# A routed expert's first rows: one expert's input gathered by one-hot matrix products on the chip instead of through memory

## The chip, the cores and the metric

The kernel runs on one core of a Trainium2 chip. A core has five engines with an instruction queue each: TensorE (PE, matrix products into PSUM; its weight loads are listed as PEld), VectorE (DVE), ScalarE (ACT), GpSimd (POOL) and SyncE (SP, which here only starts transfers). They wait for each other through semaphores. Data lies in memory (DRAM), in SBUF (128 partitions) and in PSUM, which holds the results of products. Transfers run on 16 DMA engines; SP and POOL start them.

The metric is the time of one execution on the device in microseconds (us). Everything is computed in 32-bit floating point; TensorE runs such a product of two full operands as two passes, so the profile counts two records for each.

## The reference

The model is a block of three layers over 16 sequences of 256 tokens with 128 features, 4096 tokens in all: half of a mixture of experts, an attention block, and half of the same mixture again, each on the layer-normalised stream `x` and added to it.

```
x = x + 0.5 * moe(layernorm(x))
x = x + attention(layernorm(x))      # delta rule in chunks of 32, three long convolutions, a gate
x = x + 0.5 * moe(layernorm(x))
```

What matters here is the mixture of experts, `moe`. There are 8 experts. Every token takes the two with the largest gate probability, k = 0 and k = 1. Each expert has room for 640 tokens per k; a token's place is the number of earlier tokens that chose the same expert, and a token whose place is 640 or more is dropped.

```
onehot = (eid[:, None] == experts[None, :])
pos = cumsum(onehot, axis=0) - 1 at the token's expert;  valid = pos < capacity
disp = zeros((E, capacity, D)).at[eid, pos].add(x)
gate = silu(disp @ wi_gate);  up = disp @ wi_up;  expert_out = (gate * up) @ wo
out += weight * expert_out[eid, pos]          # where valid
```

## The kernel before

**Staging.** The 4096 tokens are four groups g of 1024, each held as 128 partitions of 8 tiles n (NG = 4, NC = 8). The first mixture is layer 1, the second is layer 2. In between stands the attention phase, in which each group goes through nine or so strands (front, systems, scan, conv, gate, routing and so on). The strands are Python generators. A planner (class Weave) merges them by estimated costs and due times into one order for every engine, which is then kept as written. The last group's gate and routing are split in two halves of four tiles.

**Routing.** `choose` normalises the rows of a group into a tile `row` (128 features, the token's number, two weights), transposes them, multiplies with the gate's weights and finds the two experts. `place` turns the choices into places: VectorE sums over tiles (L462), TensorE counts over partitions in three products into `pp` (L473 to L479), and VectorE makes the number of a slot per token and k (L482 to L500: `bb`, `pos`, `full`, `place`, `send`). A slot number is 640 e + pos. Then `dispatch` (L531) writes the rows to the memory tensor `disp` at these slots: one indirect DMA by GpSimd for each tile and k. The slots were filled with zero rows beforehand. For k = 0 the eight scatters of a group go out at once. Those of the last two groups for k = 1 (`rest`) are kept for the time of the experts.

**Experts.** `experts` runs 16 steps in layer 2, k = 0 with e = 0 to 7, then k = 1. Three steps are fetched ahead. For each step SP loads the weights `we` (L233) and the slots of the expert (`fetch`, L608) as `xd`: 128 partitions of 5 rows, where slot 5 p + j is at partition p, part j. `expert` transposes the five parts on TensorE (`ptx`, L635) and copies the result to `xdT`, 128 features by 640 slots, three parts by ACT (L638) and two by DVE (L640). Then come eight pairs of products of 320 columns, `pg` and `pu` (L648, L653), with Silu on ACT and a multiplication on DVE, and 20 products back to 128 features, `py` (L668). The results are weighted to `ye` (L679) and scattered to the tokens' rows by GpSimd (L693).

**The seam.** The first expert of layer 2 can begin when the eight scatters of the last group for k = 0 have landed and SP has fetched its slots. SP has the first three weight loads, then three fetches in its queue at that point; all these fetches wait for all scatters to the tensor. GpSimd has four memsets, the eight scatters, and then the first four of `rest`. On ACT a table load for Silu (`ready`) stands before the first expert's copies. PSUM is one pool of five general banks (tag G) and three others in the attention phase, and another pool of eight for the experts.

Of the kernel before, what the change touches and what calls it, by code (L numbers as in the profile page):

```python
# [14 lines left out]
P = 128  # L15
# [143 lines left out]
def macaron_kernel(ctx: ExitStack, tc: tile.TileContext, x_in, consts, wts, w1b, wexp, out):  # L159
# [91 lines left out]

    eps_ln = one.tile([P, 1], F32, name="eps_ln")
    nc.vector.memset(eps_ln, 1e-5)
    spare = one.tile([P, 1], F32, name="spare")

# [112 lines left out]

    PAD = 4
    completed = []  # L370

    class Routing:


        def __init__(self, layer, pool, rows, wide):
# [4 lines left out]
            self.sent, self.row_ = {}, {}  # L380
            self.last, self.chained, self.final, self.waiting = None, True, None, []
            self.firsts = {2 + g: (g,) for g in range(NG)}

# [69 lines left out]
        def place(self, g, tag, t=None):  # L453
# [30 lines left out]
            full = self.small("full", nm, [2, NC, NE], 1)  # L484
            place = self.small("place", nm, [2, NC])
            send = rt.tile([P, 2, NC], I32, tag="r_send", bufs=NG, name=f"send_{nm}")
# [140 lines left out]
        def expert(self, ex, k, e, among, we, xd, xb, extra):  # L627
            nm = f"{self.layer}_{k}_{e}"
            wo = we[:, 2 * FF :].rearrange("p (f d) -> p f d", d=D)
            xdT = ex.tile([P, ESLOT], F32, tag="xdT", name=f"xdT_{nm}")  # L630
            for q, js in enumerate((range(0, 3), range(3, JS))):
                pt = psB(f"ptx_{nm}_{q}")
                w = len(js) * P
                for i, j in enumerate(js):
                    nc.tensor.transpose(pt[:, i * P : (i + 1) * P], xd[:, j, :D], ident)  # L635
                to = xdT[:, js[0] * P : js[0] * P + w]
                if q % 2 == 0:
                    nc.scalar.copy(to, pt[:, :w])  # L638
                else:
                    nc.vector.tensor_copy(to, pt[:, :w])  # L640
# [918 lines left out]
    r2_ = Routing(2, rt, held_in(rt, "row2", 2, NC * RW), wide)  # L1559

    def routing(g, part):
        yield "wait", ("chosen", *before(g, part))
        t = yield "wait", ("out", g, part)
        t = yield from r2_.choose(g, "G", t, PARTS[g][part])
        weave.mark(("chosen", g, part), t)
        if part < len(PARTS[g]) - 1:
            return
        t = yield from r2_.place(g, "G", t)

        for k in range(2 if g < NG - 2 else 1):  # L1570
            for n in range(NC):
                t = yield scatter(t)
                r2_.dispatch(g, k, [n], ABREAST[g])
        r2_.row_[g].let_go((POOL, t[1] + 3.0))

# [156 lines left out]
```

## Time and profile before

| | us |
|---|---|
| median of three runs | 1002.89 |
| lowest and highest of them | 1001.63, 1004.18 |
| the profiled execution | 1007.35 |
| its span | 1005.6 |

| engine | busy us | share of the span | instructions |
|---|---|---|---|
| PE | 843.8 | 84% | 7674 |
| PEld | 583.6 | 58% | 7674 |
| DVE | 515.4 | 51% | 1227 |
| ACT | 361.6 | 36% | 710 |
| POOL | 315.4 | 31% | 334 |

The mean granted clock of TensorE is 0.953 of full speed. By stages: layer 1's routing and experts until about 310 us, the attention phase until about 734, layer 2's experts until the end.

In the profile's rows a group or a step is named by its line in the kernel before, its engine and operation, and "out<-in" by the program's names; "x8" is how often. A row of the order in time has start, length, engine, line and operation, and in brackets how long its engine sat idle before it and what ended that. A row of the chain of waits has start, length and what. A row of busy times by stretch has the stretch, its length, then busy time and records of PE, PEld, DVE, ACT and POOL, the granted clock, the share of the DMA engines and GB/s.

### The profile page before, as it was taken

The numbers are of one execution on the slowest core, as the hardware profiler recorded it, in microseconds if no ns is written. First come the engines' busy times: TensorE is split into PE (matmuls) and PEld (weight loads), VectorE is DVE, ScalarE is ACT, GpSimd is POOL, SyncE is SP. The second block draws the span as 40 slices with busy tenths as digits, with TensorE's granted clock in tenths as the row PEclk, the third lists the DMA queues.
The fourth block names the chain that finished last, engine by engine and source line by source line (L and its number), as shares of the span: only waits on it lengthen the run. The fifth ranks groups of instructions, "written<-read, shape, count | busy, mean of one in ns | idle before, by whom it ended". The sixth has DMA issues, their size and how long they took to land.

```text
span 1005.6 us, 19291 instructions
## 1 busy us (share of the span) xinstructions
PE 843.8 (84%) x7674; PEld 583.6 (58%) x7674; DVE 515.4 (51%) x1227; ACT 361.6 (36%) x710; POOL 315.4 (31%) x334
## 2 busy tenths in 40 slices
PE   3358999999994898999989897998329999999965
PEld 1236777777773453654464464555217777877754
DVE  6434333334432379489659858856613333353522
ACT  5413222222223545445715632355512322232211
POOL 2575455523333000000032013100443553256551
PEclk9999999999997999999999999999559999999987
DMA  7923433497501411400410004000142433462610
GB/s 249 319 63 121 146 119 112 131 322 253 173 21 34 95 43 32 107 2 22 96 50 28 1 27 108 18 3 1 28 158 65 120 111 104 159 214 81 239 60 13
DMA packets 37097, 101.74 MB, mean 101 GB/s; under 512 B 9456, under 2 KB 11990, under 8 KB 37008
## 3 DMA queue, kind: packets, MB, share of 16 engines
q1 hardware_dynamic: 27152, 82.47, 26.6%
q0 software_dynamic: 9856, 18.05, 5.6%
q8 instruction: 60, 0.98, 0.4%
q14 instruction: 29, 0.24, 0.1%
HBM read 48.96 MB, written 42.39 MB: 91 GB/s over the span
## 4 chain that ended last, share of the span: by engine, by line
PE 63%; DVE 13%; issue 9%; ACT 6%; DMA 3%; another core or an unknown queue 3%; POOL 2%; SPq 1%; POOLq 0%; DVEq 0%; ACTq 0%
PE pg L648 12%; PE py L668 12%; PE pu L653 12%; PE pms L1365 7%; PE pjq L1010 2%; DMA xd<-disp 2%; DVE inv L1142 1%; DVE add L1137 1%; PE pjk L1010 1%; PE pa L1093 1%; POOL back L693 1%; PE ptx L635 1%; PE pc L1276 1%; ACT xdT L638 1%
## 5 line engine op out<-in xcount | busy, mean ns | idle before, releaser
L531 POOL DMA_INDIRECT disp<-row,send x128 | 124.4, 972 | 449.3 <-ACT tz L1159 176.2
L659 DVE TENSOR_TENSOR hT<-pu,sg 128x320 f32<-128x320 f32 (+2 forms) x256 | 124.8, 491 | 168.8 <-PE pu L653 107.8
L648 PE MATMUL pg<-xdT,we 128*128 128x320 f32 (+2 forms) x512 | 186.4, 446 | 18.4 <-ACT xdT L638 9.2
L693 POOL DMA_INDIRECT back<-ye,xd x140 | 138.8, 992 | 182.9 <-DVE ye L679 148.8
L653 PE MATMUL pu<-xdT,we 128*128 128x320 f32 (+2 forms) x512 | 182.8, 439 | 3.0 <-DVE hT L659 3.0
L658 ACT ACTIVATE sg<-pg 128x320 f32<-128x320 f32 (+2 forms) x256 | 110.8, 437 | 189.3 <-PE pg L648 121.5
L668 PEld LDWEIGHTS py<-we,hT 128*128 128x128 f32 x1280 | 148.4, 192 | 6.4 <-issue 1.4
L668 PE MATMUL py<-we,hT 128*128 128x128 f32 x1280 | 149.1, 275 | 0.9 <-issue 0.9
L648 PEld LDWEIGHTS pg<-xdT,we 128*128 128x128 f32 x512 | 96.0, 193 | 63.5 <-ACT xdT L638 15.9
L653 PEld LDWEIGHTS pu<-xdT,we 128*128 128x128 f32 x512 | 98.3, 193 | 46.4 <-DVE hT L659 5.1
L1365 PE MATMUL pms<-vlag,lagw 128*32 128x512 f32 x832 | 108.8, 595 | 0.3 <-issue 0.3
L638 ACT COPY xdT<-ptx 128x384 f32<-128x384 f32 x32 | 15.3, 478 | 172.8 <-PE ptx L635 145.1
L679 DVE TENSOR_TENSOR ye<-py,xd 128x256 f32<-128x256 f32 (+2 forms) x57 | 27.6, 485 | 90.6 <-PE py L668 85.6
L1365 PEld LDWEIGHTS pms<-vlag,lagw 128*32 128x32 f32 x832 | 29.1, 108 | 39.7 <-issue 34.4
L1142 DVE TENSOR_TENSOR inv<-inv,add 128x31 f32<-128x31 f32 (+15 forms) x124 | 42.4, 342 | 3.8
L1137 DVE TENSOR_TENSOR add<-sys,inv 128x31 f32<-128x31 f32 (+15 forms) x124 | 42.1, 340 | 3.8
L635 PE MATMUL ptx<-cst,xd 128*128 128x128 f32 x160 | 23.9, 282 | 21.3 <-DMA xd<-disp 18.2
L1291 DVE TENSOR_TENSOR ui<-pc,cst 128x512 f32<-128x512 f32 x32 | 22.0, 689 | 26.1 <-PE pc L1283 18.6
L1335 ACT COPY delta<-po 128x128 f32<-128x128 f32 x32 | 8.5, 265 | 71.2 <-PE po L1328 67.5
L635 PEld LDWEIGHTS ptx<-cst,xd 128*128 128x128 f32 x160 | 19.2, 146 | 21.6 <-issue 17.3
L1010 PE MATMUL pjk<-hT,wc 128*128 128x512 f32 x64 | 29.0, 594 | 0.6 <-DVE bt L364 0.6
L1010 PE MATMUL pjq<-hT,wc 128*128 128x512 f32 x64 | 28.7, 598 | 0.1
(227 smaller groups left out, 1051.4 us busy)
## 6 DMA issues: line engine op xcount, KB each, us to landing
we<-in_wexp_dram SPq DMA_DIRECT2D x32, 768.0 KB
disp<-empty SPq DMA_DIRECT2D x4, 2620.0 KB
xd<-disp SPq DMA_DIRECT2D x32, 327.5 KB
back<-zero SPq DMA_DIRECT2D x4, 2048.0 KB
y<-back SPq DMA_DIRECT2D x16, 512.0 KB
vlag<-vbl SPq DMA_DIRECT2D x16, 143.5 KB
vlag<-vbl SPq DMA_DIRECT2D x16, 143.4 KB
vlag<-vbl SPq DMA_DIRECT2D x16, 143.2 KB
```

What stands on the lines that cost most here:

```text
L531: sent = nc.gpsimd.indirect_dma_start(out=self.slots[k][(g * NC + n) % abreast], out_offset=bass.IndirectOffsetOnAxis(ap=send[:, k, :], ax ...
L635: nc.tensor.transpose(pt[:, i * P : (i + 1) * P], xd[:, j, :D], ident)
L648: nc.tensor.matmul(pg[:, :w], lhsT=we[:, f * P : (f + 1) * P], rhs=xdT[:, s0 : s0 + w], start=True, stop=True,)
L653: nc.tensor.matmul(pu[:, :w], lhsT=we[:, FF + f * P : FF + (f + 1) * P], rhs=xdT[:, s0 : s0 + w], start=True, stop=True,)
L658: nc.scalar.activation(sg, pg[:, :w], AF.Silu)
L659: made = nc.vector.tensor_tensor(hT[:, f, s0 : s0 + w], pu[:, :w], sg, ALU.mult)
L668: nc.tensor.matmul(py[:, i * P : (i + 1) * P], lhsT=hT[:, f, j * P : (j + 1) * P], rhs=wo[:, f, :], start=(f == 0), stop=(f == 3),)
L693: self.in_order(nc.gpsimd.indirect_dma_start(out=to, out_offset=bass.IndirectOffsetOnAxis(ap=where, axis=0), in_=what, in_offset=None, bou ...
L1010: nc.tensor.matmul(pj_.tile, lhsT=wc[:, i, k, :], rhs=hT[:, :, l0 : l0 + P], start=(k == 0), stop=(k == KQ - 1),)
L1137: nc.vector.tensor_tensor(add, sys_[:, j, k:].unsqueeze(2).to_broadcast([P, r, k]), iv[:, j, :k].unsqueeze(1).to_broadcast([P, r, k]), ALU ...
L1142: nc.vector.tensor_tensor(iv[:, k:, :k], iv[:, k:, :k], add, ALU.add)
L1365: nc.tensor.matmul(pm_[i].tile[32 * tile_ : 32 * tile_ + 32, :], lhsT=lagw[:, q, u, :], rhs=vl[:, q, :, l0 : l0 + 128], start=first, stop= ...
```

## The change

Only the input of the first expert of layer 2, for k = 0, is made in another way. Everything else, the scatters and this expert's own fetch too, stays; the fetched rows still give the weights and the token numbers of its output, no longer its features.

1. After the scatters of the third group, SP fetches expert 0's slots as they then are: rows of three groups, zeros in the last group's slots (`rows_ahead`). GpSimd writes the numbers of the slots in the order of `xdT` (an iota, the same on every partition), and DVE copies them as floats into `wc`, whose weights are no longer used.
2. When the last half of the last group has been through `choose`, TensorE transposes these five parts, and ACT copies them into a tile `xdT0` (`begin`).
3. Two products of 128x512 with no use for their result go to a bank before `place`, one behind its products (`warm`).
4. When the places are known, DVE compares the slot numbers with the place of each token of a tile: a 128x640 matrix with a one where the slot is the token's (`complete`). TensorE multiplies the tile's rows with it, and sums over the eight tiles in two banks of 384 and 256 columns. There are three buffers for the one-hot matrices, in `lagw` and `w1f`, which are no longer used either.
5. DVE adds the two sums to `xdT0`, and the expert leaves out its own transposes and copies.

The scatters of the last group stand in the order before the compares. Besides, `spare` and `eps_ln` become two columns of one tile.

```diff
-    eps_ln = one.tile([P, 1], F32, name="eps_ln")
-    nc.vector.memset(eps_ln, 1e-5)
-    spare = one.tile([P, 1], F32, name="spare")
+    pair = one.tile([P, 2], F32, name="eps_ln")
+    nc.vector.memset(pair, 1e-5)
+    eps_ln, spare = pair[:, 0:1], pair[:, 1:2]
...
+    HALVES = (range(0, 3), range(3, JS))
...
-            place = self.small("place", nm, [2, NC])
+            place = self.placed = self.small("place", nm, [2, NC])
...
-            xdT = ex.tile([P, ESLOT], F32, tag="xdT", name=f"xdT_{nm}")
-            for q, js in enumerate((range(0, 3), range(3, JS))):
+            xdT = self.begun.get((k, e))
+            if xdT is None:
+                xdT = ex.tile([P, ESLOT], F32, tag="xdT", name=f"xdT_{nm}")
+            for q, js in enumerate(() if (k, e) in self.begun else HALVES):
...
+    xdT0 = one.tile([P, ESLOT], F32, name="xdT0")
+    ahead = {}
+
+    def rows_ahead(t):
+        ahead["xd"] = xd_ = yield from wide("xd_0")
+        t = yield dma(4.0, t, xd_.free)
+        nc.sync.dma_start(
+            out=xd_.tile[:, : JS * RW], in_=disp[1][0][:ESLOT, :].rearrange("(p j) d -> p (j d)", j=JS)
+        )
+        num_ = yield from wide("slot_n")
+        t1 = yield POOL, 1.0, (num_.free,)
+        whole = num_.tile[:, :ESLOT].bitcast(I32)
+        nc.gpsimd.iota(
+            whole.rearrange("p (j q) -> p j q", q=P), pattern=[[1, JS], [JS, P]], base=0, channel_multiplier=0
+        )
+        yield "wait", ("front", NG - 1)
+        slot = ahead["slot"] = wc.rearrange("p i k d -> p (i k d)")[:, :ESLOT]
+        t1 = yield dve(ESLOT, t1)
+        nc.vector.tensor_copy(slot, whole)
...
+    def begin():
+        t = yield "wait", "ahead"
...
+        for q, js in enumerate(HALVES):
+            px_ = yield from take("G", f"px_{q}")
+            for i, j in enumerate(js):
+                t1 = yield pe(64, t, px_.free)
+                nc.tensor.transpose(px_.tile[:, i * P : (i + 1) * P], xd[:, j, :D], ident)
+            w = len(js) * P
+            t2 = yield act(w, t1)
+            nc.scalar.copy(xdT0[:, js[0] * P : js[0] * P + w], px_.tile[:, :w])
...
+    def complete(g, t):
...
+        def product(n, q, t):
...
+            nc.tensor.matmul(
+                sums[q].tile[:, :w], lhsT=row[:, n, :D],
+                rhs=hot[n % len(hot)][:, js[0] * P : js[0] * P + w], start=(n == 0), stop=(n == NC - 1),
+            )
...
+        for n in range(NC):
+            t = yield dve(ESLOT, t)
+            nc.vector.tensor_scalar(hot[n % len(hot)], slot, r2_.placed[:, 0, n : n + 1], None, ALU.is_equal)
+            for m, q in ([(n, 0), (n, 1)] if n < NC - 2 else [(n, 0)]) + (
+                [(n - 1, 1), (n, 1)] if n == NC - 1 else []
+            ):
+                ends[q] = yield from product(m, q, t)
+        for q, js in enumerate(HALVES):
...
+            nc.vector.tensor_tensor(to, to, sums[q].tile[:, :w], ALU.add)
...
+    def warm(n, to):
+        for _ in range(n):
+            yield pe(512, to.free)
+            nc.tensor.matmul(to.tile, lhsT=ident, rhs=cst[:, :512], start=True, stop=True)
...
+        if g == NG - 1:
+            yield from begin()
+            ahead["sums"] = []
+            for q in range(2):
+                ahead["sums"].append((yield from take("G", f"pz_{q}")))
+            yield from warm(2, ahead["sums"][0])
         t = yield from r2_.place(g, "G", t)
+        if g == NG - 1:
+            yield from warm(1, ahead["sums"][0])

         for k in range(2 if g < NG - 2 else 1):
             for n in range(NC):
-                t = yield scatter(t)
+                t1 = yield scatter(t)
                 r2_.dispatch(g, k, [n], ABREAST[g])
-        r2_.row_[g].let_go((POOL, t[1] + 3.0))
+        r2_.row_[g].let_go((POOL, t1[1] + 3.0))
+        if g == NG - 2:
+            yield from rows_ahead(t1)
+        if g == NG - 1:
+            yield from complete(g, t)
```

More of the change, by code (lines that the diff above doesn't have):

```diff
@@ L381, in __init__ @@
             self.last, self.chained, self.final, self.waiting = None, True, None, []
+            self.begun = {}
             self.firsts = {2 + g: (g,) for g in range(NG)}
@@ L1559, in macaron_kernel @@
     r2_ = Routing(2, rt, held_in(rt, "row2", 2, NC * RW), wide)
+    xdT0 = one.tile([P, ESLOT], F32, name="xdT0")
[16 more added lines that the diff above has]
+        nc.vector.tensor_copy(slot, whole)
+        num_.let_go(t1)
+        weave.mark("ahead", t)
@@ new lines, in begin @@
+    def begin():
+        t = yield "wait", "ahead"
+        xd_ = ahead["xd"]
+        xd = xd_.tile[:, : JS * RW].rearrange("p (j d) -> p j d", d=RW)
+        for q, js in enumerate(HALVES):
[6 more added lines that the diff above has]
+            nc.scalar.copy(xdT0[:, js[0] * P : js[0] * P + w], px_.tile[:, :w])
+            px_.let_go(t2)
+        xd_.let_go(t1)
+        room = lagw.rearrange("p q u d -> p (q u d)")
+        ahead["hot"] = [
+            room[:, :ESLOT], room[:, ESLOT : 2 * ESLOT], w1f.rearrange("p b d -> p (b d)")[:, :ESLOT]
+        ]
@@ new lines, in complete @@
+    def complete(g, t):
+        row = r2_.row_[g].tile.rearrange("p (n d) -> p n d", d=RW)
+        slot, hot, ends = ahead["slot"], ahead["hot"], {}
+        sums = ahead["sums"]
+        def product(n, q, t):
+            js = HALVES[q]
+            w = len(js) * P
+            t1 = yield pe(w, t, sums[q].free)
+            nc.tensor.matmul(
+                sums[q].tile[:, :w], lhsT=row[:, n, :D],
+                rhs=hot[n % len(hot)][:, js[0] * P : js[0] * P + w], start=(n == 0), stop=(n == NC - 1),
+            )
+            return t1
+        for n in range(NC):
[6 more added lines that the diff above has]
+        for q, js in enumerate(HALVES):
+            w = len(js) * P
+            to = xdT0[:, js[0] * P : js[0] * P + w]
+            t2 = yield dve(w, ends[q])
+            nc.vector.tensor_tensor(to, to, sums[q].tile[:, :w], ALU.add)
+            sums[q].let_go(t2)
+        r2_.begun[0, 0] = xdT0
```

## The prediction

> **What bounds the kernel now.** I read the page first. The 40 slices show TensorE busy nearly everywhere in the last quarter but for a hole around 710 to 750 us, where the granted clock, first fence, is also at half. The chain that ended last, in order of time, says what fills it:
>
> ```profile
> PEclk9999999999997999999999999999559999999987
> ```
>
> ```profile
> 733.47 0.19 DVE send L500
> 733.92 0.96 POOL disp L531
> ...
> 741.49 0.96 POOL disp L531
> 742.45 0.30 issue
> 742.75 2.81 DMA disp<-row,send
> 745.65 3.00 DMA xd<-disp
> 748.79 0.89 PE ptx L635 x3
> 749.75 0.49 ACT xdT L638
> 750.28 1.44 PE pg L648 x2
> 751.71 1.07 PE pu L653 x2
> ...
> 760.49 0.54 PE pu L653 x2
> 761.03 4.46 PE py L668 x40
> ```
>
> Start, length, piece. When the last group's places are known (the `send` instruction ends at 733.64) GpSimd issues its eight scatters one per 1.26 us, the last lands at 745.56, the expert's rows come back at 748.65, five transposes and a copy follow, and the first expert's first product starts at 750.28. That is 16.6 us in which TensorE does nothing but the transposes. Then the wake-up is paid: the same 320-column product takes 1.07 us at first and 0.54 later. From `send` to the first down product (761.03) it is 27.4 us. After that one expert follows another every 14.24 us (down products at 761.03, 775.27, 789.51), with TensorE full. The busy times by stretch say at which clock:
>
> ```profile
> 627.77:629.48 1.71, 1.71 (x4) 0.68 (x3) 1.57 (x5) 0.69 (x1) 0.94 (x1) 0.50 0.90 188
> 700.98:701.84 0.86, 0.86 (x4) 0.38 (x4) 0.27 (x1) 0.69 (x1) 0.00 (x0) 1.00 0.00 0
> 716.00:748.70 32.70, 6.74 (x30) 4.75 (x30) 8.89 (x36) 8.64 (x16) 13.99 (x17) 0.50 0.34 117
> 750.28:754.00 3.72, 3.72 (x7) 2.52 (x8) 0.92 (x2) 0.56 (x2) 1.36 (x2) 0.50 0.06 18
> 755.00:760.00 5.00, 5.00 (x20) 3.55 (x19) 2.13 (x5) 2.19 (x5) 0.00 (x0) 1.00 0.04 13
> ```
>
> The third figure from the end is the granted clock. The first two stretches are one 128x512 product each: 1.71 us at half clock, 0.86 at full.
>
> **The change part by part.** Nothing before 717 us moves: the order of every engine and the waits are the same there, and from the second expert on as well.
>
> *Removed from the path:* eight scatters, their landing, the fetch, five transposes, a copy (733.64 to 750.28). The scatters and the fetch are still issued, in the same places of their queues. They now serve only the weights and row numbers of the expert's output, needed at the first `ye`. That was at 763.7 and would come about 7 us sooner, at 756.7; the fetch lands at 748.65, so 8 us of cover. Gone, it would cost one for one.
>
> *Early rows.* One more fetch on SP, ahead of the three weight loads. It waits for the third group's scatters, the last of which goes out at 717.85 and lands 2.81 later, at 720.7; plus 3.00 it is there at 723.7. SP sits idle from 627 to 727.18, so nothing is behind it. The weight loads wait for the end of the buffers' last reader, so far `pr` at 726.7, now the early transposes at 728.0: 1.3 us later. They are 2.36 MB, and traffic falls off at about 735.5; at 737 they are still ahead of the first product.
>
> *The cell for `spare`* is joined to that for the epsilon: one memset of two columns instead of one at the very start, where VectorE idles; nothing.
>
> *Slot numbers.* An iota of 640 on GpSimd behind the scatter that ends at 718.8. The trace has 32 elements in 0.15 us and a memset of 640 in 0.63; I take 0.7, bounds 0.6 and 2. Then a copy on VectorE, 0.5 to 0.8, ahead of the residual add, which starts at 721.43 after 3.9 us of idling. Covered by 1 us; at the upper bounds it would cost about 0.4.
>
> *Early transposes and warming.* On TensorE between `pr` (ends 726.68) and the place products: five transposes (1.30 at half clock, the row at 748.79) and two 128x512 products (1.71 each at half). They end at 731.4, where the first place product started at 729.68. It had to wait until 730.56 for the counts anyway. So VectorE's `bb` comes 1.3 us late at half clock, and not at all if the clock goes up after the first of the two. I take 0.8, bounds 0 and 1.3. The two ACT copies (0.48 each) stand ahead of a table load that nobody waits for until the first expert. A third warming product lies beside VectorE's 1.84 us of place arithmetic.
>
> *One-hot places.* Eight compares of 128x640 in VectorE, three buffers. The first is on the path. The nearest rows: a 128x1024 tensor-scalar 0.69 us, one of 128x128 with a per-partition scalar 0.28; a line through the first gives 0.49, with 0.06 for the scalar 0.55. At one element per cycle, as the 128x512 two-tensor forms run (0.69), it would be 0.82. I take 0.55 and 0.10 for the handing over, as it is nearer in kind. The other seven run beside the products.
>
> *Products.* Sixteen, 640 columns for each tile, as many as one pair of 320 (2 x 0.54): 8 x 1.08 = 8.6 at full clock. How much of it runs at half clock is the main unknown. TensorE is busy from 726 on but for a hole of about 1 us when it waits for the first one-hot. In the trace the clock goes up at 754.1, after 3.8 us of unbroken work from 750.28, and it fell at 706.3, when TensorE had been busy for 0.48 of the 3.4 us before. One stretch of 3.4 us at half clock loses 1.7. I take 1.0, bounds 0 and 2.6.
>
> The Trainium skill ("TensorE: Matmul & The Clock Gate", Part 1) has the clock rise after one busy window of about 3.4 us that runs free of the program, and fall only after an idle one. By that alone nothing of the products would run at half clock and the sum would be 1.0 us better; the fall at 706.3, after half-busy work, does not agree with it.
>
> *Adding up.* Two adds from PSUM (0.56 and 0.42, the rows of `ye`); the first lies beside the last 256-column products, and the first expert's product waits for both: 0.42 and 0.2 of hand-over, 0.6.
>
> *First expert, warm:* sixteen 320-column products at 0.54, 8.75 in place of 10.75.
>
> Sum: 0.8 + 0.65 + 8.6 + 1.0 + 0.6 + 8.75 = 20.4 against 27.4: **7.0 us less**. The bounds give 8.9 and 4.5. The sum was made on the profiled execution, whose own time is 1007.35 (span 1005.6), 4.5 above the median of the runs, 1002.89. I take it off the median: **995.9**. Later waits (7.5 us before the last expert, 969.9 to 977.3) end with gathers and scatters that are issued behind earlier experts' results, so they should come 7 us sooner too.
>
> **The rivals.**
>
> *GpSimd and VectorE get in each other's way.* The scatters now run beside the one-hots.
>
> ```profile
> 58.45 0.69 DVE L759 TENSOR_SCALAR w1f<-w1f 128x1024 f32<-128x1024 f32 x1
> 58.62 1.35 POOL L531 DMA_INDIRECT disp<-row,send  x1 [0.30 <-issue]
> ```
>
> Here a scatter that met a tensor-scalar took 1.35 in place of 0.96. That direction is harmless: 0.4 on each of eight scatters is 3 us of the 8 of cover. The reverse would not be: if every one-hot first waits out a scatter, they come at 0.55 + 0.96 = 1.51. The last is ready at 745.6, 1.5 of products and the 0.6 follow, the gain is 4.5 and the time 998.4; with a whole scatter pitch (1.26 + 0.55 = 1.81) it is 1000.5. Against it: no VectorE row beside scatters is longer than its like elsewhere, but none of those is a tensor-scalar that starts inside a scatter.
>
> The Trainium skill ("SBUF — State Buffer", Who interferes with whom) states just this: whichever of the two starts first holds the shared port for its whole instruction. The row at 58.62 agrees for one direction; no row shows the other.
>
> *The other side: the one-hots set the pace and are dear.* Place: VectorE between `send` and the adds. Break-even is a pitch of 2.15 us (the last one-hot 4.5 us later than at 1.51); at 2.6 the kernel is 3 us slower, about 1006. It takes the slow form (0.82) and more than a whole scatter's wait each time. Little speaks for it.
>
> *The early rows are late.* TensorE takes its work in order, so the place products stand behind the early transposes. If the fetch lands after 726.7 instead of at 723.7, all is late one for one; at 733.7 the gain is gone: 1002.9. The 3.00 us of the same fetch speak against it.
>
> *Given back later.* If the waits from 890 to 980 hang on a queue that doesn't move with the first expert, the time stays near 1002.9. The chain there does hold 21.8 us of "issue" and transfers of 7 to 8.7 us; but none is issued ahead of an expert's result.
>
> **How the numbers follow.** Forecast 0.62; the two engines in each other's way 0.16; late rows 0.05; given back 0.10; dear one-hots 0.07. A measurement of this kernel can tell 0.3%, 3 us, from no change. Faster: 0.62 and 0.15 of the second, 0.77; slower 0.08; the rest, 0.15, within. The range runs from 993.0 (8.9 off, and a little for the phase of the clock, which in the profiled execution was a kind one for the kernel before) to 1000.5 (the dearer form of the second case): 0.78 or so.
>
> **What would show it.** In the changed kernel: early transposes straight behind `pr`; `bb` up to 1.3 us later; eight one-hots of about 0.55 us; products at 1.08 a tile, with the granted clock at 1.0 from some point before 738; the first expert's product at about 745 and the first down product at about 754; scatters of 1.0 to 1.5 us; the second expert without a wait. It would be wrong if a one-hot starts only when a scatter ends, if the clock is at half past 742, or if the hole before the last expert grows by what was won.

## The result, and the profile after

The changed kernel takes 993.58 us (median of four runs, 991.1 to 994.65) where the kernel before takes 1002.95 (1001.63 to 1004.18): the ratio is 0.9903, 95% interval 0.9879 to 0.9927, or 9.4 us less. The forecast was 995.9, 7.0 less.

The two profiled executions have spans of 1005.6 and 990.9 us, 14.7 apart. Of these, 5.1 us lie ahead of the change: the last output's transposes (`pt_o`) already start at 717.50 before and at 712.42 after, when of the new work only the joined memset has run, and from there to the last gate products (`pr`, at 726.03 and 720.94) it is 8.53 in both. e2 below, which runs the old code up to there, has `pr` at 720.63, on another chip; so executions of the same code differ by this much, and nothing says that the 5 us are the change's. Everything below is told from the start of `pr`. From there the first down product comes after 34.83 us before and 26.16 after: 8.67 less. The tenth expert's down products come 8.8 sooner (163.1 and 154.3), the last product ends 9.0 sooner (267.3 and 258.3).

The chain of the changed kernel that ended last, in order of time (start, length, piece):

```profile
721.60 1.26 PE px L1599 x5
722.86 2.91 PE pz L1646 x4
...
728.20 0.17 DVE send L502
728.38 0.48 DVE lagw L1628
728.85 0.04 issue
728.90 8.88 PE pz L1620 x32
737.78 0.63 issue
738.41 0.78 PE pg L652 x2
...
747.26 4.46 PE py L672 x40
```

`px` are the early transposes, `pz L1646` the useless products (two records to a product), `pz L1620` the one-hot products. Where the chain before went through eight scatters, a fetch and transposes, it now goes through one compare and sixteen products. From the end of `send` (728.37) to `py` it is 18.9 us, before it was 27.4. The 1.44 and 1.07 of the first expert's first products are gone too: 0.78 and 0.54.

The busy times by stretch (us, then TensorE, its weight loads, VectorE, ScalarE, GpSimd; the third figure from the end is the granted clock):

```profile
720.00:724.00 4.00, 3.33 (x17) 2.00 (x16) 2.03 (x10) 1.87 (x2) 1.03 (x2) 0.50 0.05 13
724.00:728.00 4.00, 3.29 (x11) 1.39 (x9) 2.74 (x12) 2.42 (x6) 1.31 (x3) 0.86 1.00 363
728.00:732.00 4.00, 3.10 (x11) 2.20 (x12) 2.90 (x7) 0.00 (x0) 2.74 (x3) 1.00 0.62 252
```

The clock goes up at 725.1, during the second useless product and 3.8 us ahead of the first one-hot product. Before, it went up at 754.1, in the middle of the first expert. Nothing of the sixteen products runs at half clock.

The absolute times below differ by chip (the kernel before takes 1007.9, 1010.7, 1008.4 and 980.0 us beside the four later sets of runs), so each run is told as a ratio to the kernel before on its own chip, and the traces from the start of `pr`. One table holds the readings, in us after the start of `pr`, each a start in the timeline except where it says end:

| run | `send` ends | first one-hot product | first expert's first product | first down product | tenth expert's down product | last product ends |
|---|---|---|---|---|---|---|
| before | 7.61 | | 24.25 | 34.83 | 163.1 | 267.3 |
| after | 7.43 | 7.96 | 17.47 | 26.16 | 154.3 | 258.3 |
| after again (e5) | 7.19 | 7.71 | 17.22 | 25.91 | 154.2 | 255.9 |
| after again (e11) | 7.19 | 7.71 | 17.22 | 25.91 | 155.4 | 256.6 |
| no useless products (e1) | 7.61 | 8.13 | 19.26 | 27.95 | 156.1 | 261.3 |
| before + useless products (e2) | 7.61 | | 24.01 | 32.73 | 160.9 | 266.8 |
| compares twice (e3) | 7.20 | 8.31 | 19.46 | 28.15 | 156.3 | 260.5 |
| compares twice, then `send` (e9) | 15.62 | 8.23 | 17.99 | 28.60 | 162.9 | 263.4 |
| products twice (e4) | 7.19 | 7.72 | 25.84 | 34.53 | 162.7 | 267.0 |
| no completion (e6) | 8.44 | | 7.57 | 16.26 | 152.0 | 256.6 |
| split sum, last gap filled (e7) | 7.21 | 7.73 | 17.31 | 25.99 | 154.5 | 258.3 |
| the same, filled ahead (e8) | 6.96 | 7.49 | 17.06 | 25.75 | 154.0 | 257.8 |
| filled ahead alone (e10) | 6.96 | 7.49 | 18.48 | 27.17 | 156.1 | 256.5 |
| filled through (e12) | 6.96 | 7.48 | 16.99 | 25.68 | 153.9 | 246.3 |

From the first down product to the tenth expert's it is 128.2 to 128.5 us, nine times 14.24 and a little, except in e10 and e11 (129.0 and 129.5) and in e6 and e9, whose edits show there. Behind the tenth, nearly the same code takes 100 to 106 us from run to run, and 92 in e12 on the fast chip. Part of that is the idle time of TensorE before the last expert: 7.5 us in the kernel before, 8.7, 2.7 and 4.6 in the three profiles of the changed kernel, 0.35 in e12. So the last column differs by waits near the end that the change does not touch, and a gain of a microsecond has to be read at the seam.

### The profile page after: what moved, and what is told of

It is laid out like the page before. It is cut to its first block, busy times and chain, and to the rows that moved or that the text cites. A ratio compares the mean times of both kernels' runs of the same rounds, so it can differ in the third digit from the quotient of the medians.

```text
span 990.9 us, 19386 instructions
## 1 busy us (share of the span) xinstructions
PE 853.6 (86%) x7712; PEld 590.5 (60%) x7712; DVE 520.6 (53%) x1237; ACT 362.2 (37%) x711; POOL 318.0 (32%) x335
## 4 chain that ended last, share of the span: by engine, by line
PE 64%; DVE 13%; issue 9%; ACT 6%; another core or an unknown queue 3%; DMA 2%; POOL 1%; SPq 0%; POOLq 0%; ACTq 0%; DVEq 0%
PE pg L652 12%; PE pu L657 12%; PE py L672 12%; PE pms L1369 7%; PE pjq L1014 2%; DMA xd<-disp 2%; DVE inv L1146 1%; DVE add L1141 1%; PE pjk L1014 1%; PE pa L1097 1%; POOL back L697 1%; PE pc L1280 1%; PE pyo L1550 1%; PE po L1332 1%
## 5 line engine op out<-in xcount | busy, mean ns | idle before, releaser
L642 ACT COPY xdT<-ptx 128x384 f32<-128x384 f32 x31 | 14.8, 478 | 154.2 <-PE ptx L639 125.3
L1097 PE MATMUL pa<-kqq,kh 128*32 128x64 f32 x1024 | 25.1, 220 | 3.5 <-issue 3.5
L344 PE MATMUL pt_r<-cst,row 128*128 128x128 f32 x64 | 16.2, 385 | 13.5 <-ACT row L333 13.1
```

The source lines that it names most:

```text
L1097: nc.tensor.matmul(pa[b * CH : (b + 1) * CH, c0 : c0 + 2 * CH], lhsT=kh[:, i % 2, h, at0 : at0 + CH], rhs=kqq[:, 0 : q_ + 1 : q_, n * P + ...
```

## The experiments

**How much is path, how much is clock: e1 and e2.** e1 is the changed kernel without its useless products:

```
-            yield from warm(2, ahead["sums"][0])
         t = yield from r2_.place(g, "G", t)
-        if g == NG - 1:
-            yield from warm(1, ahead["sums"][0])
```

> The changed kernel without its three useless products (nothing of the result is left out). Theory 1, they hold the clock up and cost nothing themselves: between the early transposes (end 722.9 in the profile of the changed kernel) and the first one-hot product (728.9) TensorE then has only the three place products, 0.6 us, and the clock is at half when the products begin. It went up 3.8 us after TensorE began on full work in the kernel before (750.28 to 754.1); 3.8 us at half lose 1.9, two windows of 3.4 us at worst 2.6 more or less: 1.7 to 2.8 us slower than the changed kernel, 995.3 to 996.4, and the first tiles take 2.16 us instead of 1.08. Rival 2, the transposes and the work before them (TensorE was busy for 3.33 of the 4 us from 720) raise the clock by themselves: within 0.5 us of 993.6. Rival 3, the useless products push the places back: the send instruction ends earlier by more than 0.3 us after the gate products, and the kernel is faster.

Ratio 0.9941 (0.9918 to 0.9963). The timeline of its TensorE (start, busy time, line, operation; in brackets the idle time before and what ended it), and the stretch before the products:

```profile
732.43 4.04 PE L1620 MATMUL pz<-lagw,row 128*128 128x384 f32 x8 [2.56 <-DVE lagw L1628]
736.31 1.24 PE L1620 MATMUL pz<-w1f,row 128*128 128x384 f32 x4
```

```profile
728.80:732.20 3.40, 1.04 (x4) 0.93 (x4) 2.09 (x8) 1.53 (x3) 0.01 (x1) 0.50 1.02 427
```

TensorE works 1.04 of 3.4 us, the clock stays at half, and the first two tiles take 4.04 us where they took 2.42. The first down product comes 1.79 us later than with the useless products (27.95 against 26.16): theory 1. Of this, 1.6 is the half clock in the products and 0.2 the place products, which run at half clock too. `send` ends at 7.61 as before, so the useless products do not push the places back; they bring them forward by 0.2. Rivals 2 and 3 fall.

e2 puts sixteen useless products into the hole of the kernel before:

```
         r2_.row_[g].let_go((POOL, t[1] + 3.0))
+        if g == NG - 1:
+            to = yield from take("G", "pz_0")
+            for _ in range(16):
+                t1 = yield pe(512, to.free)
+                nc.tensor.matmul(to.tile, lhsT=ident, rhs=cst[:, :512], start=True, stop=True)
+            to.let_go(t1)
```

> The kernel before, with sixteen useless 128x512 products behind the last place products: TensorE is kept at work through the hole while the rows go through memory, and nothing else is changed. Theory 1, the gain has two parts, a shorter path and a warm clock: the first expert's sixteen products of 320 columns take 8.75 in place of 10.75, the five transposes 0.3 to 0.5 less: 2.0 to 2.5 us faster than the kernel before, about 1000.5, and some 7 us of the measured 9.4 belong to the path through memory. Rival 2, the clock is most of the gain (the wake-up is dearer than it reads): 996 or less. Rival 3, the useless products run into the transposes or the clock falls again before them: no gain, 1003 or more.

Ratio 0.9968 (0.9944 to 0.9993). Its timeline on TensorE:

```profile
726.04 16.40 PE L1579 MATMUL pz<-cst 128*128 128x512 f32 x32
743.51 0.74 PE L635 MATMUL ptx<-cst,xd 128*128 128x128 f32 x5 [1.07 <-DMA xd<-disp]
744.64 0.81 PE L648 MATMUL pg<-xdT,we 128*128 128x320 f32 x2 [0.39 <-ACT xdT L638]
```

The first down product comes 2.10 us sooner than in the kernel before (32.73 against 34.83), as theory 1 said. So of the 8.67 us of the change, 6.9 come without any useless product (34.83 to 27.95) and 1.8 with them; and useless products alone, without any change of path, were worth 2.1. The 6.9 are not all path: the one-hot products raise the clock too, and the first expert takes 8.69 us in e1 where it took 10.59 before. From the end of `send` to that expert's first product, e1 takes 11.65 us in place of 16.63. So the two parts do not simply add: the shorter way to the first expert is worth 5.0 us where neither kernel has useless products, and the first down product comes 6.6 us sooner where both have them (32.73 to 26.16).

**Is the stretch the path: e4.** Each product is done twice, so that the last group's rows count double in the first expert:

```
-            t1 = yield pe(w, t, sums[q].free)
-            nc.tensor.matmul(
+            for again in range(2):
+                t1 = yield pe(w, t, sums[q].free)
+                nc.tensor.matmul(
...
-                rhs=hot[n % len(hot)][:, js[0] * P : js[0] * P + w], start=(n == 0), stop=(n == NC - 1),
...
+                    start=(n == 0 and not again), stop=(n == NC - 1 and again == 1),
```

> The changed kernel with each of the sixteen one-hot products done twice into the same sum, so that the rows of the last group enter the first expert doubled and its output is not the reference's. Theory 1, the products are the path and all that follows hangs on them rigidly: 8 more tiles at 1.08: 8.6 us slower, 1002.2, first down product 8.6 later, and the hole before the last expert as it was. Rival 2, the stretch has slack behind it (the hole of 8.7 us before the last expert, or the fetches): it takes part of it up: 994 to 999.

Ratio 1.0002 (0.9977 to 1.0026). The products take 17.49 us in place of 8.88, the first down product comes 8.4 later than in the first profile of the changed kernel (8.6 later than in e5 and e11), the tenth expert's 8.4 and the last product's end 8.7. Theory 1: one for one, and the gain is gone, as the sum says.

**What the compares cost and what holds them: e3 and e9.** In e3 every compare is issued twice:

```
             nc.vector.tensor_scalar(hot[n % len(hot)], slot, r2_.placed[:, 0, n : n + 1], None, ALU.is_equal)
+            t = yield dve(ESLOT, t)
+            nc.vector.tensor_scalar(hot[n % len(hot)], slot, r2_.placed[:, 0, n : n + 1], None, ALU.is_equal)
```

> The changed kernel with every compare done twice, the same result (nothing is left out). Theory 1, one-hots of 0.55 us are covered by products of 1.08 a tile and are not held by scatters: twice 0.55 and hand-over is 1.15 a tile, just over the products; the eighth pair is ready 9.2 us after the send instruction, the last three products (1.5) follow: last product 10.7 after it, where it was 9.4: 1.0 to 1.6 us slower than the changed kernel, about 995. Rival 2, VectorE and the scatters of GpSimd do get in each other's way, and it only did not show while VectorE was idle half the time: every second compare waits out a scatter (0.96), 1.6 to 2.1 a tile, 5 to 9 us slower, 998 to 1002. Rival 3, there is more cover than I read (the products wait for something else): within 0.5 us of 993.6.

Ratio 0.9932 (0.9907 to 0.9957); the first down product 2.0 to 2.2 us later than in the changed kernel. That is less than rival 2 and more than theory 1. The timelines of VectorE and GpSimd in that run say why:

```profile
736.11 0.76 DVE L1628 TENSOR_SCALAR w1f<-wc,place 128x640 f32<-128x640 f32 x1
736.91 0.56 DVE L1630 TENSOR_SCALAR w1f<-wc,place 128x640 f32<-128x640 f32 x1
737.38 0.76 DVE L1628 TENSOR_SCALAR lagw<-wc,place 128x640 f32<-128x640 f32 x1
```

```profile
735.62 0.96 POOL L533 DMA_INDIRECT disp<-row,send  x1 [0.30 <-issue]
736.89 0.96 POOL L533 DMA_INDIRECT disp<-row,send  x1 [0.30 <-issue]
```

The pairs fall into step with the scatters: 736.11, 737.38, 738.64, 739.91, every 1.265 us, and the scatters start every 1.265. From the third pair on, one compare of each takes 0.76. To see whether the scatters do this, e9 keeps the doubled compares and moves the `send` instruction, and with it the scatters, behind the last compare:

```
+            if self.layer == 2 and g == NG - 1:
+                self.unsent = send, place, g
+            else:
...
+        send, place, _ = r2_.unsent
+        ts = yield dve(16, t)
+        nc.vector.tensor_tensor(
+            send, place, beyond[:, g].unsqueeze(1).to_broadcast([P, 2, NC]), ALU.min
+        )
+        ahead["sent"] = ts
         for q, js in enumerate(HALVES):
...
             yield from warm(1, ahead["sums"][0])
+            yield from complete(g, t)
+            t = ahead["sent"]
...
-        if g == NG - 1:
-            yield from complete(g, t)
```

> The kernel with every compare done twice, but with the send instruction of the last group, and so its eight scatters, behind the last compare on VectorE (nothing of the result is left out). It asks what made a pair of compares 1.265 us there. Theory 1, the scatters that run beside them hold VectorE for about 0.2 us each (the compares of 0.76): with no scatter beside them every compare takes 0.55 to 0.56, a pair 1.13 to 1.16, and the last product ends 1.0 to 1.2 us earlier than in that run, 17.6 to 17.9 us after pr in place of 18.8. Rival 2, the compares wait for the products' buffers or for TensorE's use of the same data: pitch 1.26 and compares of 0.76 stay without scatters. On the other side the fetch behind the scatters ends about 9.4 us later, 32 to 34.5 us after pr, where the second expert's transposes stand at about 32: they wait for 0 to 3 us, and the kernel is 0 to 3 us slower than with the scatters in their place; if the rows had more slack than I read, it is 0.5 to 1 us faster.

Ratio 0.9982 (0.9944 to 1.002). VectorE with no scatter beside it:

```profile
743.43 0.55 DVE L1631 TENSOR_SCALAR w1f<-wc,place 128x640 f32<-128x640 f32 x1
744.02 0.55 DVE L1633 TENSOR_SCALAR w1f<-wc,place 128x640 f32<-128x640 f32 x1
744.49 0.55 DVE L1631 TENSOR_SCALAR lagw<-wc,place 128x640 f32<-128x640 f32 x1
```

All sixteen compares take 0.55, a pair 1.05, less than the 1.13 expected. The last product ends 17.36 us after `pr`, 1.46 sooner than in e3. So a scatter does hold a compare, by 0.21 us, not by its 0.96. In the changed kernel itself VectorE is idle for about 0.5 us ahead of each compare from the fourth on, and the hold (0.79 once, at 734.59) costs nothing.

The second half of the expectation concerned the rows. `send` and the scatters come 8.4 us later here. The rows are in time all the same: the transposes of the second and the third expert start as the down products ahead of them end. What is late is something else. The first expert takes 10.6 us to its down product in place of 8.7, with waits of ScalarE and VectorE inside it, and the third expert's down product comes 5 us late (62.1 us after `pr`, where two steps of 14.24 from the first would make 57.1), because ScalarE copies its transposes only 3.3 us after they end and the clock falls meanwhile (785.8 to 789.2). The profile does not name what that copy waited for:

```profile
781.60 0.71 PE L642 MATMUL ptx<-cst,xd 128*128 128x128 f32 x5
785.58 0.48 ACT L645 COPY xdT<-ptx 128x384 f32<-128x384 f32 x1 [8.35 <-remote]
```

GpSimd's queue is some 8 us behind at that point; that this is the cause is not shown. By the tenth expert the run is 6.6 us behind e3, more than the 0 to 3 that I expected.

**What is late next: e6.** The completion is left out, so the last group's rows are missing from the first expert:

```
-            yield from complete(g, t)
+            for held in ahead["sums"]:
+                held.let_go(t)
+            r2_.begun[0, 0] = xdT0
```

> The changed kernel without compares, one-hot products and adds: the last group's rows are missing from the first expert's input, so its output is not the reference's. It asks what is late next behind the completion. Theory 1, TensorE can begin the first expert once the places are done (6.5 us after pr in place of 17.5), 10 to 11 us sooner, but the fetch behind the scatters still ends about 23 us after pr, and the second expert's transposes, at 30.8 after pr in the changed kernel, then wait for it: 6.5 to 8 us faster than the changed kernel, with an idle TensorE of about 3 us before the second expert. Rival 2, nothing is close behind: the whole 10 to 11 us come off. Rival 3, the scatters themselves or the first expert's output on GpSimd hold all up: less than 5 us.

Ratio 0.9895 (0.9836 to 0.9954), not to be told from the 0.9897 of the changed kernel on the same chip (e5), where theory 1 expected 6.5 to 8 us less and rival 3 under 5. The first down product comes 9.65 us sooner than in e5. Of that the second expert's down product keeps 3.0 (37.2 in place of 40.2 us), the tenth's 2.2 (152.0 in place of 154.2), and the end nothing. The timeline of TensorE before the second expert, and a stretch there:

```profile
753.33 1.33 PE L639 MATMUL ptx<-cst,xd 128*128 128x128 f32 x5 [3.46 <-DMA xd<-disp]
```

```profile
751.00:754.00 3.00, 0.67 (x3) 0.68 (x4) 0.89 (x2) 0.00 (x0) 0.00 (x0) 0.53 1.00 393
```

Theory 1 named the place: the second expert's rows, fetched behind the scatters, are there 25.5 us after `pr`. It had the price of that too low. The wait is 3.5, and while TensorE waits the clock falls (751.1 to 758.0), so that 4.7 us of the second expert's work run at half and lose 2.3 more. So behind the change as it is there were, by the trace, about 2 us left to win by a shorter completion, not 9. This run also has the case that the prediction feared for the places: the clock goes up only at 734.1, the two useless products take 3.62 in place of 2.91, and `send` ends at 8.44, 0.8 later than in the kernel before.

**Can more be had: e5, e7, e8, e10, e11, e12.** e5 and e11 are the changed kernel once more.

> The changed kernel once more, unaltered, as the base for the other runs on this chip and for a second profile of the stretch. Theory 1: from the last gate products (pr) on everything stands where it stood in its first profile: send ends 7.4 us after their start, the first product 8.0, the first expert's product 17.5, the first down product 26.2 after it, and the clock is at full before the first product. Rival 2, the first profile met a kind phase of the clock: up to two windows of the products run at half here, and the first down product comes 27 to 29 us after pr.

> The changed kernel unaltered, on the same chip as the run with the useless products ahead of the seam, to set the two side by side, and a third profile of the stretch: first down product 25.9 to 27.3 us after pr (26.2 and 25.9 in the two profiles so far; 27.3 if the clock goes up as late as in the run without the completion, where the places came 1.2 us later).

e5 and e11 have ratios of 0.9897 (0.9866 to 0.9929) and 0.9923 (0.9889 to 0.9958); in both the first down product comes at 25.91. Three profiles of the changed kernel, with the rise of the clock at three distances (4.2, 3.1 and 3.6 us after `pr`), show no half clock in the products.

e7 keeps the sum in two halves of 320 columns in two tiles, and fills the gap before the last expert:

```
-    xdT0 = one.tile([P, ESLOT], F32, name="xdT0")
+    HS = ESLOT // 2
+    xdT0 = [one.tile([P, HS], F32, name=f"xdT0_{q}") for q in range(2)]
...
+                rhs=hot[n % len(hot)][:, q * HS : q * HS + w], start=(n == 0), stop=(n == NC - 1),
...
             else:
+                pw = psA(f"pw_{nm}") if self.final else None
+                for _ in range(8 if self.final else 0):
+                    nc.tensor.matmul(pw, lhsT=ident, rhs=cst[:, :512], start=True, stop=True)
                 for f in range(4):
```

> The changed kernel with two more steps, result complete. First, the sum is kept in two halves of 320 columns in tiles of their own, so that the first expert's first product waits for the first add alone, which lies beside the last products: 0.5 to 0.6 us less (the idle 0.63 us before it goes). Second, eight useless 128x512 products in the idle 7.5 to 8.9 us before the last expert. Theory 1, the clock fell there because TensorE idled: with 6.9 us of work the half-clock stretch of 7 to 10 us in the last expert goes, 3.4 to 5 us less; together 4 to 5.5 us faster than the changed kernel. Rival 2, the last expert hangs on GpSimd's scatters and not on TensorE: the products end sooner and the kernel does not, under 1.5 us. Rival 3, the idle stretch is shorter than 6.9 us in some executions and the useless products are in the way: slower by up to 2 us.

Ratio 0.9895 (0.9841 to 0.9949): not to be told from e5 on the same chip. Neither step did what it was for. The split: the first expert's first product still starts 0.10 us after the *second* add, though it reads the first half alone. It waits on VectorE's semaphore until that add is done. Read off the kernel, the reason is that a new set of PSUM banks begins at the experts and its first user waits for the last reader of the old set; no run tests this. The gap: the clock did stay at full to the last down products, and the last expert's first product came as soon as the useless ones ended, but the fourth product then waited. The timeline of ScalarE:

```profile
969.85 0.48 ACT L642 COPY xdT<-ptx 128x384 f32<-128x384 f32 x1 [11.93 <-PE pw L720]
974.30 0.87 ACT L663 ACTIVATE sg<-pg 128x384 f32<-128x384 f32 x2 [3.97 <-remote]
```

ScalarE comes out of an idle stretch that ends on nothing the profile names ("remote") at 974.3, and the last product ends no sooner (258.3). That is rival 2 in kind: the last expert hangs on another engine, if not on GpSimd's scatters.

e8 adds useless products ahead of the seam; e10 has these alone:

```
+        final = g == NG - 1 and part == len(PARTS[g]) - 1
+        if final:
+            pw_ = yield from take("G", "pw")
...
         nc.vector.tensor_reduce(ws, wl3, AX.X, ALU.add)
+        if final:
+            for _ in range(6):
+                nc.tensor.matmul(pw_.tile, lhsT=ident, rhs=cst[:, :512], start=True, stop=True)
...
+            if final:
+                for _ in range(2):
+                    nc.tensor.matmul(pw_.tile, lhsT=ident, rhs=cst[:, :512], start=True, stop=True)
+                pw_.let_go(t1)
             xh = x[:, g, 4 * half : 4 * half + 4, :].rearrange("p n d -> p (n d)")
```

> As the run before it, and eight more useless 128x512 products ahead of the seam, result complete: six in the 8.5 us in which TensorE has nothing while VectorE does the last part's gating, two behind the last output products. Theory 1, the clock then is at full from about 4 us into them, and the output products, the row transposes and the gate products, which lie on the path in turn with VectorE and ScalarE (1.09, 1.5, 1.13, 0.65 us at half clock), take half: 1.5 to 2.2 us less ahead of pr, together 5.5 to 7.7 us faster than the changed kernel. Rival 2, at half clock six such products are 10.3 us and run into the transposes of the output: no gain or a loss of up to 2 us against the run before it. Rival 3, the clock falls again in the gaps between these steps (0.7 to 2.8 us idle): no gain.

> The changed kernel with the eight useless products ahead of the seam alone (six while VectorE does the last part's gating, two behind the last output products), result complete: the only one of the three further steps that shortened its stretch in a trace, 8.52 to 6.89 us from the transposes of the last output to the gate products. Theory 1: 1.5 to 1.9 us faster than the changed kernel on the same chip, with the same 25.8 us from pr to the first down product; in the times 0.15 to 0.2%, at or under what they can tell. Rival 2, it is taken back by the phase of the clock later: no difference, or within 0.5 us of the changed kernel.

Ratios 0.9894 (0.9857 to 0.9932) and 0.9912 (0.988 to 0.9943), not to be told from the changed kernel on the same chips (0.9897 and 0.9923); the 5.5 to 7.7 us that theory 1 of e8 expected in all did not come. In e8 the stretch from the last output's transposes to `pr` does take 6.89 us in place of 8.52, the part that theory 1 had for it. In e10 it takes 7.81, and the products lose what was won, rival 2:

```profile
733.13 3.90 PE L1630 MATMUL pz<-lagw,row 128*128 128x384 f32 x8 [1.61 <-DVE lagw L1638]
```

```profile
716.10:719.50 3.40, 1.02 (x6) 0.71 (x6) 1.57 (x7) 3.02 (x7) 2.67 (x4) 0.94 0.14 46
729.70:733.10 3.40, 1.57 (x6) 0.74 (x6) 2.48 (x10) 1.75 (x3) 0.21 (x1) 0.95 1.02 425
```

The clock fell twice, at 719.1 and 732.8, each time at the end of 3.4 us in which TensorE had worked for about half or less (0.34 and 0.52 by the trace; the two rows lie 0.4 us later). e12 puts one more useless product into each of these two stretches:

```
-            for _ in range(6):
+            for _ in range(7):
...
-            yield from warm(1, ahead["sums"][0])
+            yield from warm(2, ahead["sums"][0])
```

> The kernel with the useless products ahead of the seam, with two more: seven instead of six in the first gap, and two instead of one behind the place products, result complete. In the profiles so far every fall of the granted clock follows a stretch of 3.4 us in which TensorE was busy for 0.55 or less, and it held through stretches of 0.59 and more; in the run with six and one it fell twice, after 0.34 and 0.52, and the one-hot products then took 10.4 us in place of 8.9. Theory 1, the busy share of the 3.4 us decides: two products of 0.86 us add 0.25 to each of these two stretches, the clock stays at full from about 713 on whatever the phase, 6.9 us from the transposes of the last output to pr (8.5 in the changed kernel) and 25.7 to 25.9 us from pr to the first down product: 1.6 us faster than the changed kernel by the trace. Rival 2, something else than the busy share lets it fall: it falls again before the first expert, and pr to the first down product is 27 us or more, or the first stretch 7.8 us. Rival 3, the added products run into the work behind them: the first one-hot product comes later than 7.5 us after pr.

Ratio 0.9872 (0.9846 to 0.9898), the lowest of all, though its interval overlaps that of the changed kernel. Its TensorE:

```profile
713.00 1.96 PE L1656 MATMUL pz<-cst 128*128 128x512 f32 x4
715.71 2.42 PE L1630 MATMUL pz<-lagw,row 128*128 128x384 f32 x8 [0.75 <-DVE lagw L1638]
```

The two products fit in front of the first one-hot product, the clock stays at full from 696 to 958.9 us, and the first down product comes at 25.68. The first stretch takes 7.49 us, between e8 and the changed kernel, because the row transposes came 0.6 later behind the output products than in e8. What held them is the change's own copy of the slot numbers, which stands ahead of the residual add on VectorE and waited for the iota:

```profile
703.52 0.49 DVE L1596 CAST wc<-slot_n 128x640 f32<-128x640 int32 x1 [2.65 <-POOL slot_n L1589]
703.92 0.68 DVE L1566 TENSOR_TENSOR x<-x,pyo 128x512 f32<-128x512 f32 x1
```

The output products end at 703.29; the add starts 0.63 us behind them, where it started 0.03 to 0.04 behind in all other runs. With the 0.2 to 0.5 us behind `pr` the run is 1.3 to 1.5 us better than the changed kernel by the trace: theory 1, nearly at its size. This is one profile on another chip, and it shows that the two products were enough here. The rule that the expectation took as its ground, a fall after 0.55 or less and none after more, does not hold through the traces (last section).

## Why the prediction was right, and where it was off

The mechanism is the one forecast: the first expert no longer waits for memory, all experts behind it move with it, and the kernel is faster by just under 1%. The sum from `send` to the first down product, term by term:

| term | forecast | measured (first profile) |
|---|---|---|
| `send` later than before | +0.8 (0 to 1.3) | -0.18 |
| first one-hot and hand-over | 0.65 | 0.53 |
| products | 8.6 | 8.88 |
| half clock in them | 1.0 (0 to 2.6) | 0 |
| add and hand-over | 0.6 | 0.63 |
| first expert | 8.75 | 8.85 |
| sum | 20.4 | 18.71 |

Against 27.39 that is 8.68 where 7.0 was forecast. Nearly the whole difference is two terms, and both are the clock; they err the same way, so nothing cancelled by luck. *Early transposes and warming* had the two useless products delay the places by 0.8. In ten of eleven profiles with these two products they did not: the clock is up before the place products, which are busy for 0.38, 0.39 and 0.29 us in the timeline where they were for 0.77, 0.80 and 0.45, and `bb` starts 5.0 to 5.4 us after `pr` where it was 5.6. In the eleventh (e6) the delay was 0.84. The prediction named this case (no delay if the clock rises after the first useless product), but its bounds for the term, 0 to 1.3, left out that the places could come sooner. *Products* allowed 1.0 for half clock; it was 0 with the useless products in every profile but e10, where it was 1.5, and 1.6 without them (e1), all within its bounds of 0 to 2.6. When the clock rises is chance in part: 3.1 to 4.2 us after `pr` in the three profiles of the changed kernel, 6.2 in e6. The values taken were too cautious.

The measured 9.4 us and the 8.7 of the trace agree within the interval of the times (7.3 to 12.1 us).

*One-hot places*: 0.55 us, as taken from the line through two other forms. *Early rows*: the early transposes follow `pr` without a wait, and the weight loads are issued at 722.93, 0.8 later than before in this count, and their traffic falls off at about 730.5, eight us ahead of the first expert. *Slot numbers*: the iota takes 0.69, the copy 0.49, and the residual add starts 0.04 after its products. The cover was 1.4 us in the first profile and 0.6 in e11; in e12, where the useless products shorten the stretch ahead, it was gone and the copy cost 0.6. *Later waits*: the hole before the last expert moved with the rest in the first profile (7.5 us before, 8.7 after), and was shorter in the two others (2.7 and 4.6); what sets its length is open.

*Removed from the path* said that the scatters and the fetch had 8 us of cover. That looked at the first expert's own output only. The rows of the second and third expert come by the same fetches: starting the first expert 9.65 us sooner kept 2.2 (e6). The change as it stands does not touch this bound; one step further it would have been the next limit. In the other direction, scatters 8.4 us later cost 6.6 (e9), but there the rows were in time and the waits were others.

Of the rivals, *GpSimd and VectorE get in each other's way* is real as a mechanism and false in price: 0.21 us a scatter (e3 against e9), where it needed 0.96. It stays hidden since a compare with it, 0.76, is shorter than the 1.08 of the products. The prediction held against it that no tensor-scalar of the kernel before starts inside a scatter; four do (at 58.25, 59.30, 903.01 and 914.71), none of them longer than its like, but all of 128 columns or fewer, so they could not have given this price. The Trainium skill ("SBUF — State Buffer", Who interferes with whom) has whoever comes first hold the shared port for its whole instruction; by that a pair beside a scatter would take 2.1 us in e3 (0.55 twice and 0.96), and it took 1.265. *Dear one-hots*: no, 0.55 and a pitch of 1.08. *Early rows late*: no. *Given back later*: no; the tenth expert's gain, 8.8, is that of the first, 8.7.

## What to carry to other kernels

Where an expert's, a tile's or a stage's last inputs are on the chip already, a product with one-hot places is a way to gather them without memory; here 10.0 us of compare, products and add replaced 16.6 us of scatter, landing, fetch and transposes. Before a burst of products that sets the path, useless ones in TensorE's waits can keep the clock up: 1.8 us here, and they delayed the places in one profile of eleven (e6, by 0.84). And when a step is taken off the path, look for everybody who eats from the same transfer, not only the one that was moved.

## What was not expected of the hardware

**The clock can fall after half-busy stretches, not only idle ones.** In each of the 14 profiles all changes of the granted clock lie whole multiples of 3.41 us apart. Around the seam (690 to 765 us) and at the end (from 955) it falls 41 times, each time after 3.41 us in which TensorE was busy for 0.55 or less, sixteen times for between 0.44 and 0.55. Each rise follows a stretch with 0.85 or more, though four of 0.82 to 0.91 did not raise it yet. The Trainium skill ("TensorE: Matmul & The Clock Gate", Part 1) has a window of that length, running free of the program, and a clock that falls after an idle window; the length agrees with these runs, the fall does not. By that rule the prediction had the products at full clock and the sum 1.0 us better, and so it came; but the useless products keep these stretches busy, so this does not bear the rule out. The busy share is no threshold either. In the same parts of the traces, with the stretches counted from the last rise, the clock held through 14 that were busy for 0.43 to 0.55 (0.52 in the one that ends at 702.4 in e5, 0.43 in the one that ends at 964.9 in e10). And between 500 and 585 us it also fell after stretches of up to 0.77 (the one that ends at 579.8 in e4). What else decides is open.

**A scatter holds a compare of VectorE by 0.21 us** in e3, and by 0.24 at most in the profiles of the changed kernel, with 16 of 16 compares at 0.55 when no scatter is near (e9); and the pairs lock to the scatters' own pitch of 1.265.

**Still open:** what ends the waits of ScalarE and VectorE before the last expert (in the first profile of the changed kernel ScalarE's copy starts 8.4 us after the transposes that it reads) and in e9 before the third. The profile calls it "remote", its length differs from execution to execution, and it limits what a warm clock can win at the end.
